# Attention of four batches and scores of the next four in one block on TensorE

## The chip, the cores and the metric

The kernel runs on one core of a Trainium2 chip. The metric is the device time of one execution in microseconds. It is the median of several runs. One further execution was taken by the hardware profiler, and the views quoted below are of that one. Engines are named as in the profile: PE is TensorE (PEld its weight loads), DVE is VectorE, ACT is ScalarE, POOL is GpSimd, SP is the engine whose queue issues nearly all DMAs.

## What is computed

Two layers over 128 batches of a 128 x 512 matrix, all in fp32. The first takes a maximum over the features of adj x; the second is attention with 8 heads of 64 features, masked by the adjacency, with a projection and a layer norm.

```python
# layer 0: A = C - b = adj @ x, so out = max(0, max(A, axis=-1) + b); one value a row
x = layernorm(x + layer0(x))
# layer 1
q, k, v = split(x @ w_qkv)                    # 8 heads of 64
attn = softmax(where(adj == 0, -inf, q @ k.T * 64 ** -0.5))
o = (attn @ v) @ w_proj + b_proj
x = layernorm(x + o + layernorm(o) * ln_gamma + ln_beta)
```

(In the reference layer 0 adds A at one feature to C - A at another; C - A is the bias b, since A and C use the same adjacency.)

## The kernel before

**Tiling.** Four batches are a group (G = 4, 32 groups). A batch is 128 rows, so one batch's matrix fills the 128 partitions. The projections q and k together, v, and the output projection o of a group are done as "units": a unit is a matrix product of 512 tokens by 512 columns in seven products of half size (Strassen's scheme in Winograd's form) instead of eight. `product(i)` (L171) is eight matmuls of 128 x 128 weights by 256 columns. Products 1, 6 and 7 go into PSUM bank b1, one added on top of the other, 2 into b2, 5 and 3 into b3, 4 into b4. `snap(k)` (L184) is a copy of b1 by ScalarE after product 1, 6 or 7; `result(half, col)` (L202) is an addition by VectorE of a bank and a snap, into SBUF: (0, 0) reads b2, (0, 1) b3, (1, 0) b4, and (1, 1) b3, before product 3 is added to it. The sums that the scheme needs of the operands are made by GpSimd (`x_sums`, `o_sums`, `weight_sums`), in the beginning also by VectorE.

**Attention of a batch.** `scores(b)` (L396) is 16 matmuls with 64 rows of the array, in pairs, even heads into one bank and odd heads into another; `softmax_max` (L407) scales and masks the two banks into an SBUF tile s and takes the maximum of each head; `softmax_exp` (L425) is eight exponentials on ScalarE; `softmax_div` (L439) divides; `prob_transpose` and `prob_write` (L447, L457) transpose in blocks of 32 and write to DRAM, and `prob_read` (L466) reads back into a tile pT with the transposition finished. `attend(b)` (L482) is 16 matmuls with 64 columns of the array, in pairs, into one bank; `attend_copy` (L496) copies that bank out by ScalarE.

**The main loop** (L806) has 60 steps; step p does two batches, a = 2p and b = 2p + 1. Each step begins on TensorE with a block, `attend(a - 2)`, `attend(b - 2)`, `scores(a)`, `scores(b)`. After that come the seven products of `first` (a half of the q and k columns of the next group), two layer-0 products `l0_mm` and the seven products of `second`. In even steps (ph = 0) `second` is the output projection of the group before; in odd steps it is v of the next group. Product 3 of a unit is issued in the course of the next unit (`before.product(3)`). All 8 PSUM banks are in use: b1 to b4 by the units, pss0 and pss1 by scores and later in the step by `l0_mm`, po and pa by attention and by the second batch's scores.

**The order.** It is written out by hand: every instruction is pinned to the program's order on its engine, so each engine runs its instructions in exactly the order of the source. A tile with a tag has that tag's slots; an instruction that first writes a new tile in a slot waits until the last reader of the old one is done. After the loop the last eight batches are written out one by one; the beginning, before the loop, does layer 0 of the first groups.

## Time and profile before

| what | us |
|---|---|
| median of three runs | 1952.45 |
| lowest and highest | 1952.12, 1953.76 |
| the profiled execution, its own time | 1953.87 |
| span of its profile | 1951.6 |
| mean granted clock of TensorE | 0.998 |

In a view of the timeline a line has the start, the time to the last end, engine, line of the kernel, operation, what it writes and reads, shapes, how many in a row, and in brackets how long the engine was idle before, and what ended this. Ends of matmuls are modelled, as these are pipelined: what one costs is seen from one start to the next. The lines named L77 and L74 are those of helpers, so groups are told apart by their tiles: b_qk, b_v and b_o are the banks of the three kinds of unit, po an attention, pss scores, pa a layer-0 product, pt a transpose on TensorE.

| group | number | mean ns |
|---|---|---|
| masking of scores, a bank (L411) | 256 | 682 |
| division of a softmax (L77) | 128 | 1978 |
| copy of an attention bank (L501), median | 128 | 586 |
| snap of q and k (L186) | 192 | 586 |
| result of q and k (L77) | 256 | 675 |

### The profile page before, as it was taken

Reading aid. Unit: us, or ns where it says so; the run is one execution under the profiler, and the core shown is the slowest. Engines: PE = TensorE matmul, PEld = TensorE weight load, DVE = VectorE, ACT = ScalarE, POOL = GpSimd, SP = SyncE. Lnnn points to the kernel's source line nnn. Section 1 sums busy time; section 2 is a strip of 40 time slices with the busy share of each in tenths; the row PEclk is TensorE's granted clock in tenths of the full one; section 3 lists DMA queues with packets and bytes.
Section 4 is the critical chain, followed back from the end, with each engine's and each line's share of the span. In section 5 each row is a group of like instructions: output and inputs, shape, how many; then the busy total and the mean of one; then the engine's idle time right before and its main releaser. Section 6 shows DMA issues by size and latency. Waiting matters only on the chain.

```text
span 1951.6 us, 33053 instructions
## 1 busy us (share of the span) xinstructions
PE 1937.1 (99%) x11541; PEld 1638.4 (84%) x11541; DVE 1560.6 (80%) x2514; ACT 1065.2 (55%) x3095; POOL 1293.7 (66%) x823
## 2 busy tenths in 40 slices
PE   9999999999999999999999999999999999999998
PEld 6888888888888888888888888888888888888885
DVE  6767878778788787787887877877878778778787
ACT  3544655545546555555465555554655555546566
POOL 6336666767667676676776676766767666767648
PEclk9999999999999999999999999999999999999999
DMA  7647566575665665756756657657667576675574
GB/s 221 167 127 182 146 190 169 166 206 151 174 193 157 190 170 165 206 151 174 198 156 187 175 161 205 161 166 193 159 186 179 167 195 162 166 204 154 157 227 141
DMA packets 444934, 341.74 MB, mean 175 GB/s; under 512 B 276832, under 2 KB 378336, under 8 KB 444768
## 3 DMA queue, kind: packets, MB, share of 16 engines
q1 hardware_dynamic: 444336, 338.85, 63.6%
q8 instruction: 91, 1.49, 0.3%
q10 hardware_dynamic: 432, 0.79, 0.2%
q14 instruction: 75, 0.61, 0.1%
HBM read 172.82 MB, written 166.72 MB: 174 GB/s over the span
## 4 chain that ended last, share of the span: by engine, by line
PE 95%; DVE 2%; POOL 1%; ACT 1%; DMA 0%; issue 0%; SPq 0%; POOLq 0%; ACTq 0%; DVEq 0%
PE b_qk L74 40%; PE b_v L74 19%; PE b_o L74 18%; PE pss L74 6%; PE po L74 6%; PE pa L74 5%; DVE st_mv_last L261 0%; POOL zl L77 0%; DMA x<-in_x_dram 0%; ACT s L430 0%; POOL s_o L77 0%; DVE amax L297 0%; DVE mv_last L262 0%; DVE o L77 0%; DVE pu L451 0%
## 5 line engine op out<-in xcount | busy, mean ns | idle before, releaser
L74 PE MATMUL b_qk<-s_x,wqk 128*128 128x256 f32 x2048 | 473.6, 379 | 1.0 <-DVE qk L77 0.8
L74 PEld LDWEIGHTS b_qk<-s_x,wqk 128*128 128x128 f32 x2048 | 388.8, 190 | 55.4 <-DVE qk L77 1.5
L430 ACT ACTIVATE s<-s,nmax 128x128 f32<-128x128 f32 x1024 | 396.2, 391 | 5.3 <-DVE nmax L423 5.3
L74 PE MATMUL b_qk<-x1T,wqk 128*128 128x256 f32 x1536 | 360.2, 384 | 0.1
L74 PEld LDWEIGHTS b_qk<-x1T,wqk 128*128 128x128 f32 x1536 | 287.9, 191 | 45.5 <-issue 1.0
L77 POOL TENSOR_TENSOR z<-z,ga_bc 128x1024 f32<-128x1024 f32 x58 | 164.6, 2837 | 167.0 <-ACT z L284 167.0
L275 POOL TENSOR_SCALAR rs_mv<-mv 128x6 f32<-128x6 f32 (+2 forms) x61 | 14.8, 242 | 385.8 <-DVE mv L262 385.8
L77 DVE TENSOR_TENSOR s<-s,rec 128x1024 f32<-128x1024 f32 x128 | 253.2, 1978 | 4.4
L186 ACT COPY u_qk<-b_qk 128x512 f32<-128x512 f32 x192 | 112.5, 586 | 243.3 <-PE b_qk L74 242.4
L74 PE MATMUL b_v<-wv,s_x 128*128 128x256 f32 x1024 | 237.0, 379 | 0.0
L74 PE MATMUL b_o<-wp,s_o 128*128 128x256 f32 x992 | 229.6, 379 | 0.2 <-ACT u_o L186 0.2
L74 PEld LDWEIGHTS b_v<-wv,s_x 128*128 128x128 f32 x1024 | 194.4, 190 | 26.9 <-ACT u_v L186 0.4
L411 DVE SCALAR_TENSOR_TENSOR s<-pss,mask 128x512 f32<-128x512 f32 x256 | 164.1, 682 | 61.4 <-PE pss L74 61.2
L74 PEld LDWEIGHTS b_o<-wp,s_o 128*128 128x128 f32 x992 | 188.2, 190 | 26.4 <-issue 0.8
L77 DVE TENSOR_TENSOR qk<-b_qk,u_qk 128x512 f32<-128x512 f32 x256 | 167.9, 675 | 48.5 <-PE b_qk L74 44.5
L77 POOL TENSOR_TENSOR x<-x,be_bc 128x1024 f32<-128x1024 f32 x64 | 181.3, 2835 | 33.1 <-DVE rec L441 27.4
L430 ACT ACTIVATION_READ_ACCUMULATOR s<-s,nmax 128x1 f32 x1024 | 194.6, 190 | 0.0
L77 DVE TENSOR_TENSOR v<-b_v,u_v 128x512 f32<-128x512 f32 x127 | 86.1, 679 | 133.8 <-PE po L74 128.9
L186 ACT COPY u_o<-b_o 128x512 f32<-128x512 f32 x91 | 53.3, 586 | 238.7 <-PE b_o L74 238.7
L186 ACT COPY u_v<-b_v 128x512 f32<-128x512 f32 x95 | 55.7, 586 | 233.1 <-PE b_v L74 233.1
L74 PE MATMUL b_v<-wv,x1T 128*128 128x256 f32 x768 | 176.5, 379 | 0.0
L74 PEld LDWEIGHTS b_v<-wv,x1T 128*128 128x128 f32 x768 | 145.8, 190 | 32.3 <-issue 13.9
(129 smaller groups left out, 3399.6 us busy)
## 6 DMA issues: line engine op xcount, KB each, us to landing
hop<-pu SPq DMA_DIRECT2D x128, 512.0 KB, 3.6
pT<-hop SPq DMA_DIRECT2D x512, 128.0 KB, 3.7
spill<-x SPq DMA_DIRECT2D x64, 512.0 KB, 4.8
x<-in_x_dram SPq DMA_DIRECT2D x62, 512.0 KB, 4.4
xhop<-xt SPq DMA_DIRECT2D x248, 128.0 KB, 2.3
x1T<-xhop SPq DMA_DIRECT2D x248, 128.0 KB, 3.9
xr<-spill SPq DMA_DIRECT2D x59, 512.0 KB, 3.6
out_dram<-xr SPq DMA_DIRECT2D x58, 512.0 KB, 4.1
```

The costliest lines, as they stand in the source:

```text
L74: pin(nc.tensor.matmul(*args, **kwargs))
L77: pin(eng.tensor_tensor(dst, a, b, op))
L186: pin(nc.scalar.copy(t, self.banks[1]))
L275: pin(nc.gpsimd.tensor_scalar(rs[:, :n], mv[:, :n, 1], EPS, None, ALU.add))
L411: nc.vector.scalar_tensor_tensor(s[:, par], pss[b][par], SCALE, mask.unsqueeze(1).to_broadcast([P, NP, P]), ALU.mult, ALU.add,)
L430: nc.scalar.activation(prob[b][:, i], prob[b][:, i], AF.Exp, bias=nmax[b][:, i : i + 1], accum_out=psums[b][:, i : i + 1],)
```

## The change

In steps with p > 1 the block comes in even steps only. `group_block` issues the attention of the four batches of the group before, each into the next of the banks po, pa, pss0, pss1, and then the scores of all four batches of the new group, into b2 and b1, b4 and the first free bank, two free banks, and the last free bank and b2 again. `group_mask` masks all four on VectorE, with the maximum of the first batch between. Odd steps take the maxima of the last two batches, from the s tiles that were masked before. The step p = 2 attends two batches only, since p = 1 keeps its own block. After the loop, the last even step has the same block, and the scores of L - 5 and L - 4 in the middle of it are gone.

In an even step `first.product(2)` comes after `before.product(3)`, the two results there change places, the exponentials of b come after `first.snap(2)`, and `first.result(1, 1)` and `(1, 0)` come before `softmax_div(b)`.

Tiles: v has 4 slots (2 groups) instead of 2; s and pT share 4 slots (they had 2 each); the second half of q and k has 2 slots instead of 3; the transposed x (xt) has one instead of two. The last two s tiles lie in the place of the q and k weights.

In the beginning the sums of the weights are issued in another order (two of them ahead of a statistic), batch 2 is normalised by VectorE instead of ScalarE, product 2 comes before the transposes of batches 2 and 3, the results of the first unit come before a group of statistics, and products 4 and 5 of the next unit change places.

```diff
-    def softmax_max(b):
-        s = sb.tile([P, 2, NP, P], F32, tag="s", name=f"s_{b}", bufs=2)
-        for par in range(2):
+    def softmax_mask(b, order=(0, 1), place=None):
+        s = place or sb.tile([P, 2, NP, P], F32, tag="s", name=f"s_{b}", bufs=4)
+        for par in order:
...
+    def softmax_max(b):
+        if b in pss:
+            softmax_mask(b)
         nmax[b] = small.tile([P, H], F32, tag="nmax", name=f"nmax_{b}")
...
+    weight_sums(wqk, 0, HE, 2)
+    mv = stats("first_2", ("y", 2), ("y", 3), fused=1)
+    rs, _ = stat_of.pop(("y", 2))
+    pin(nc.vector.tensor_scalar(xs[2], xs[2], mv[:, 0, 0:1], rs, ALU.subtract, ALU.mult))
+    l0_norm(3)
...
     cur.product(1)
     cur.snap(1)
+    cur.product(2)
     for f in range(2, G):
         l0_transpose_pe(f)
-    cur.product(2)
...
+    before.snap(3)
+    l0_add(2 * G - 1)
+    before.result(1, 1)
+    before.result(1, 0)
     stats("second", *(("y", f) for f in range(G, 2 * G)))
     weight_sums(wv, 0, HE)
-    before.snap(3)
-    before.result(1, 1)
-    before.result(1, 0)
...
+    def group_block(old):
+        a = old[-1] + 1
+        free = ["po", "pa", "pss0", "pss1"]
+        for t in old:
+            attend(t, free[0])
+            attend_copy(t)
+            free.append(free.pop(0))
+        banks = ("b2", "b1"), ("b4", free[0]), (free[1], free[2]), (free[3], "b2")
+        for k in range(G):
+            scores(a + k, banks[k])
+
+    def group_mask(a):
+        softmax_mask(a)
+        softmax_mask(a + 1)
+        softmax_max(a)
+        softmax_mask(a + 2)
+        softmax_mask(a + 3, (1, 0))
...
-        if p > 0:
-            attend(a - 2)
-            before.snap(3)
-            attend_copy(a - 2)
-            attend(b - 2, "pa")
-            attend_copy(b - 2)
+        before.snap(3)
+        if p == 1:
+            for t, tag in ((0, "po"), (1, "pa")):
+                attend(t, tag)
+                attend_copy(t)
             scores(a)
             scores(b, ("po", "pa"))
-        else:
-            before.snap(3)
+        if p > 1 and ph == 0:
+            group_block(range(2 if p == 2 else a - G, a))
         before.result(1, 1)
...
         if p > 0:
             softmax_max(b)
             first.product(1)
             first.snap(1)
-            first.product(2)
+            if p == 1 or ph:
+                first.product(2)
             softmax_exp(a)
...
+        if p > 1 and ph == 0:
+            before.product(3)
+            first.product(2)
+            before.result(0, 1)
+            first.result(0, 0)
+        else:
+            first.result(0, 0)
+            before.product(3)
+            before.result(0, 1)
...
         if p > 0:
             first.snap(3)
-        else:
+        if p == 0 or ph == 0:
             first.result(1, 1)
             first.result(1, 0)
         softmax_div(b)
```

## The prediction

> **What bounds the kernel now.** I read the page first (sections 1 and 4), then the timeline of TensorE over one step of the main loop, then the other engines at the same place, then the waits of TensorE.

> ```profile
> PE 1937.1 (99%) x11541; PEld 1638.4 (84%) x11541; DVE 1560.6 (80%) x2514; ACT 1065.2 (55%) x3095; POOL 1293.7 (66%) x823
> PE 95%; DVE 2%; POOL 1%; ACT 1%; DMA 0%; issue 0%; SPq 0%; POOLq 0%; ACTq 0%; DVEq 0%
> ```

> TensorE is busy 1937.1 of 1951.6 us, and 95% of the chain that ended last is its own. Of its waits the longest is one of 1.7 us at the beginning; in the loop there are none. So only two things count: TensorE time that goes away, and waits that the new order gives to TensorE. The first is found in an even step (p even, its block at 645.44):

> ```profile
> 643.62 1.89 PE L74 MATMUL b_v<-wv,s_x 128*128 128x256 f32 x8
> 645.44 1.97 PE L74 MATMUL po<-pT,v 128*64 128x128 f32 x32
> 647.34 2.06 PE L74 MATMUL pss<-qk 64*128 64x128 f32 x32
> 649.32 3.72 PE L74 MATMUL b_qk<-x1T,wqk 128*128 128x256 f32 x16
> 652.88 1.89 PE L74 MATMUL b_v<-wv,s_x 128*128 128x256 f32 x8
> ```

> Eight projection matmuls take 1.726 us from start to start (649.32 to 652.88 is one switch and 16 of them; 16 without a switch take 3.45). From 643.62 + 1.726 = 645.35 to 652.88 - 3.45 = 649.43 the two attentions and two scores take 4.08 us. Inside, they run in pairs, 0.110 and 0.112 us apart (22 and 24 records in two short windows: (1.37 - 0.27)/10 and (1.51 - 0.28)/11):

> ```profile
> 615.74 1.37 PE L74 MATMUL po<-pT,v 128*64 128x128 f32 x22
> ...
> 617.69 1.51 PE L74 MATMUL pss<-qk 64*128 64x128 f32 x24
> ```

> 16 x 0.1093 + 16 x 0.1117 = 3.54 us (the means to one more digit). The other 0.55 us are the three changes of tile shape: 128x128 to 128x64, to 64x128, and back.

> [...] The trace agrees: 0.14, 0.20 and 0.20 us. [...] the division of a softmax (two SBUF inputs) takes 1.23 us alone, and 1.88 beside GpSimd, where it ends 1.08 us after GpSimd's instruction does; GpSimd's product then takes 3.34 instead of 2.37:

> ```profile
> 656.36 1.27 POOL L77 TENSOR_TENSOR s_o<-oT,s_o 128x512 f32<-128x512 f32 x1
> 657.59 3.34 POOL L77 TENSOR_TENSOR z<-z,ga_bc 128x1024 f32<-128x1024 f32 x1
> 661.00 3.23 POOL L77 TENSOR_TENSOR z<-z,o 128x1024 f32<-128x1024 f32 x1
> 664.31 2.35 POOL L77 TENSOR_TENSOR xr<-xr,z 128x1024 f32<-128x1024 f32 x1
> 666.62 2.35 POOL L77 TENSOR_TENSOR x<-x,be_bc 128x1024 f32<-128x1024 f32 x1
> ```

> ```profile
> 61.29 1.23 DVE L77 TENSOR_TENSOR s<-s,rec 128x1024 f32<-128x1024 f32 x1
> ...
> 656.83 1.88 DVE L77 TENSOR_TENSOR s<-s,rec 128x1024 f32<-128x1024 f32 x1
> ```

> **Part 1, fewer blocks.** Before, p = 2 to 59 have 58 blocks; after, the even ones alone, 29. Each block removed saves 0.55: -15.9 us. The scores that stood alone in the end (1853.51) join a block too: in and out of that shape, about -0.4. All other matmuls stay.

> **Part 2, the odd step loses its cover.** Products 1, 6 and 7 of a unit share bank b1. The last thing that an even step gives TensorE is second.product(7); the first in an odd step from p = 3 on is now first.product(1), into the same bank, which ScalarE must first copy out (before.snap(3)). Until now the block lay between the two. Elsewhere the two products with the adjacency (l0_mm) or, without these, the order (2, 1) separate them.

> ```profile
> 645.60 0.59 ACT L186 COPY u_v<-b_v 128x512 f32<-128x512 f32 x1 [4.60 <-PE b_v L74]
> ```

> Product 7 starts its last matmul at 645.13, which ends at 645.51; the copy runs 645.60 to 646.19. TensorE could start at 645.35, and starts about 0.1 after the copy: 0.94 us of wait. After a wait the first matmul is slower, too. Both can be seen in the two waits of this kind in the trace: it goes on 0.05 us after VectorE's 70.29 and 0.14 after ScalarE's 1917.20, and its eight matmuls take 0.10 and 0.08 more:

> ```profile
> 70.35 1.99 PE L74 MATMUL b_qk<-s_x,wqk 128*128 128x256 f32 x8 [0.23 <-DVE v L77]
> ...
> 1917.34 1.97 PE L74 MATMUL b_o<-wp,s_o 128*128 128x256 f32 x8 [0.24 <-ACT u_o L186]
> ```

> 1.03 us (0.97 to 1.09; a wait can't gain) x 29 odd steps = +29.9 us. Queued behind it is the whole TensorE stream; nothing else hides it.

> **Part 3, the even step.** The new block takes 4 x (0.875 + 0.893) + 0.55 = 7.6 us, so first.product(1) starts at 652.87 instead of 649.43. Do its banks come free? snap(3) ends 646.19, result(1,1) and (1,0) at 647.5 (V is held for two groups, so they no longer wait for the attention); b4 is wanted at 650.1. The four attention copies end by 649.9; their banks are wanted from 650.1 on. The first mask starts 650.25 and frees b2 at 650.9; the fourth score wants it at 651.9. VectorE then does eight masks (0.605 apart) and the first maximum (1.14): the last but one mask frees b2 at 655.7, and first.product(2), moved behind before.product(3) (652.87 + 1.83 + 1.73), wants it at 656.4. It fits by 0.7 us; if VectorE were later, each us beyond costs 29 us.

> Then TensorE runs products 2, 6, 5, 4, 7; the last matmul of 7 starts at 664.84, snap(3) ends at 665.9. Here is the second new wait. first.result(1,1) and (1,0) are moved ahead of softmax_div(b), so VectorE, done with the first batch (about 664.9), waits for snap(3), and all the following comes after: two results 1.17, reciprocal 0.20, division 1.26, transpose 1.17, two statistics of o 1.61, two l0_max 1.66, first.result(0,1) 0.68. From 665.94 that is 673.69, and second.product(5), into the bank b3 that this result reads, is wanted at 664.84 + 8.84 = 673.68 (the same distance as 661.30 to 670.14 now). So it just fits if the division is undisturbed. It is disturbed: GpSimd's chain keeps its times up to 657.59; there z x gamma, no longer beside a division, ends at 659.95, z + o at 662.4 (it holds the first division, ready at 660.4, back to 663.5), the sum into xr starts then and ends 665.9, and l0_beta runs 665.95 to 668.3. The second division, due at 667.3, ends at 668.3 + 1.08 instead of 668.55: 0.8 to 0.9 late; 1.4 if the first division comes before z + o (they are 0.35 apart). With 0.16 for restarting and slower first matmul: 1.0 or 1.5, taken 1.1, bounds 0 and 1.6. The order before had results behind both transposes, with VectorE at work from 654 to 667.7 and 0.87 spare. For p = 4 to 58 (p = 2 has no o statistics): 28 x 1.1 = +30.8 us (0 to 45).

> In the odd step VectorE has four masks less, and by the same sum no later bank is late.

> **Part 4, the beginning.** Now the transposes of batches 2 and 3 wait 1.71 us for their normalisation, and in the clock window after that gap TensorE is granted half speed: 16 matmuls from 18.68 take 4.91 instead of 3.45.

> ```profile
> 17.25 1.63 PE L327 MATMUL pt<-ident,x 128*128 128x128 f32 x8 [1.71 <-ACT x L284]
> 18.68 5.07 PE L74 MATMUL b_qk<-x1T,wqk 128*128 128x256 f32 x16
> ```

> ```profile
> 14.79:18.20 3.41, 1.65 (x10) 0.98 (x9) 0.60 (x3) 1.82 (x3) 2.99 (x5) 1.00 1.06 377
> 18.20:21.62 3.42, 3.42 (x11) 2.84 (x10) 3.06 (x4) 0.17 (x1) 3.34 (x3) 0.50 0.74 237
> 1939.90:1943.32 3.42, 2.47 (x7) 0.92 (x6) 3.32 (x8) 2.52 (x4) 2.99 (x7) 1.00 0.35 129
> ```

> (Columns: length, busy time of TensorE, weight loads, VectorE, ScalarE, GpSimd, then clock.) Product 2, which needs neither, now fills the gap; product 4 starts when the transposes are copied, near 19.45 instead of 21.86: -2.4. Statistics moved behind result(1,1) take away the 0.79 wait at 36.6 and its slow first matmul, -0.9. I take -3.0 (-1 to -4). GpSimd's sums are the same eight.

> **At nothing:** the mask and copy counts are unchanged; SP issues the same DMAs in the same queue order, and an even step's probabilities now have a step more to land. One xt buffer is refilled a step later, 30 us against 2.3 to landing. The s and pT tiles share four buffers: each pT follows its own s. The end I take as moved as a whole, 0 (+-1).

> **Sum** against the profiled execution's own 1953.87 (span 1951.6): -15.9 - 0.4 + 29.9 + 30.8 - 3.0 = +41.4, so 1995.3. It lies 1.4 above the median of the runs, 1952.45; for that the forecast is **1994**.

> **Rivals.**
> - Only the wait for b1: GpSimd is over a us later or earlier than I place it, or VectorE has slack. For it: 0.87 spare now. Against: l0_beta covers the due time by 1.3 us before and 1.0 after. -19.3 + 29.9: **1963**.
> - Faster: the odd step's start costs nothing, because something that I overlook keeps b1 free, and the b3 wait stays under 0.1. Place: second.product(7) to first.product(1); it decides where that wait is below 0.55 us. Against: a copy of 0.59 us after the last matmul's end is needed in any case. -19.3: **1933**.
> - The clock: [...] 1.65 us busy in such a window cost half the clock of the next, 2.47 did not; a wait of 1.1 leaves 2.3, which no run shows. If it trips in every second step: 29 x 1.7 more, **2043**.
> - The b3 wait without that for b1: 1964.

> **Chances.** Both waits 0.52 (own range 1984 to 2008), b1 alone 0.26, clock 0.09, faster 0.08, b3 alone 0.03, about even 0.02. Faster or slower is told from 0.2% (3.9 us) on: faster 0.08, within 0.02, slower 0.90. The range 1958 to 2010 takes in the first two and the last but one; the clock and the faster case are left out.

> **What would show it.** Right: in the waits of TensorE, b_qk behind ACT u_o 29 times, about 0.9 each, and b_o behind DVE qk 28 times, about 1; 31 blocks of po; first.product(2) behind no DVE s. Wrong: no wait where an odd step begins, or a b2 wait in the new block, or clock windows of 0.5 in the loop.

## The result and the profile after

The changed kernel takes 2061.28 us (four runs, 2057.43 to 2061.96) where the kernel before takes 1952.73 beside it: 1.0552 times as long, with a 95% interval from 1.0539 to 1.0565. It was forecast slower, at 1994 with 2010 as the upper end; the loss of 108.6 us is 2.6 times the 41.4 us that the sum had. The first two lines are from the page of the profiled execution after (2061.92 us, span 2060.1); the next two are from its list of TensorE's waits (total us, number, longest).

```profile
PE 1968.9 (96%) x11541; PEld 1661.0 (81%) x11541; DVE 1564.4 (76%) x2515; ACT 1056.5 (51%) x3094; POOL 1262.0 (61%) x823
...
PE 78%; DVE 17%; ACT 2%; POOL 1%; issue 1%; DMA 0%; ACTq 0%; POOLq 0%; SPq 0%; DVEq 0%
```

```profile
PE b_o L75 <- DVE qk L78: 55.2, 28, 2.0
PE b_qk L75 <- ACT u_o L187: 21.7, 29, 1.0
```

Both forecast waits are there, in the forecast places and numbers: 29 at the beginning of the odd steps, behind ScalarE's copy, and 28 in the even steps, behind the result that frees b3. VectorE now holds 17% of the chain, which was 2%. But TensorE is also busy 32 us longer than before, with the same 11541 matmuls and less switching. The timeline of TensorE from the end of an even step to the beginning of an odd one shows all three:

```profile
700.78 1.89 PE L75 MATMUL b_o<-wp,s_o 128*128 128x256 f32 x8
704.63 2.67 PE L75 MATMUL b_o<-wp,s_o 128*128 128x256 f32 x8 [1.96 <-DVE qk L78]
707.09 2.94 PE L75 MATMUL b_o<-wp,oT 128*128 128x256 f32 x8
709.87 1.89 PE L75 MATMUL b_o<-wp,s_o 128*128 128x256 f32 x8
712.49 3.72 PE L75 MATMUL b_qk<-x1T,wqk 128*128 128x256 f32 x16 [0.73 <-ACT u_o L187]
```

Product 6 begins at 700.78, so product 5 could follow 1.73 later, at 702.50; it starts at 704.63. That is a wait of 2.13 us, not 1.0 to 1.5 (the bracket says 1.96 because a matmul's end is modelled later than the next could start; read starts against starts). Products 5 and 4, 2.67 and 2.94 long instead of 1.89, run partly at half clock. Then product 7 starts at 709.87, product 1 of the odd step could start at 711.60, and starts at 712.49: 0.89 us.

The half clock is in the table of stretches (length, busy time of TensorE, weight loads, VectorE, ScalarE, GpSimd, granted clock, DMA share, GB/s). The stretches are windows of 3.41 us on the grid on which the clock's records of this profile change:

```profile
702.39:705.80 3.41, 1.45 (x7) 1.06 (x6) 3.30 (x8) 1.98 (x3) 0.00 (x0) 1.00 0.97 254
705.80:709.21 3.41, 3.41 (x9) 2.66 (x8) 2.63 (x8) 0.00 (x0) 0.67 (x2) 0.50 1.09 291
1149.53:1152.94 3.41, 1.49 (x7) 1.34 (x8) 3.27 (x10) 1.98 (x3) 0.00 (x0) 1.00 0.95 235
1152.94:1156.36 3.42, 3.42 (x18) 3.02 (x17) 2.35 (x7) 0.00 (x0) 1.00 (x2) 1.00 1.08 311
```

The first window holds the whole wait, and the next one runs at half clock; the third holds 1.92 us of a wait as long, cut by the window's edge, and the clock stays. Twenty of the 28 waits are followed by a window at half clock. Such a fall of the clock after a wait is called a trip below. From one block of attentions to the next, a pair of steps takes 64.32 us with a trip and 62.63 us without, so a trip costs 1.69 us.

Why is the wait twice what was forecast? VectorE's timeline before the result, and GpSimd's beside it:

```profile
694.75 1.29 DVE L78 TENSOR_TENSOR qk<-b_qk,u_qk 128x512 f32<-128x512 f32 x2 [2.08 <-ACT u_qk L187]
695.96 0.19 DVE L448 RECIPROCAL rec<-sums 128x8 f32<-128x8 f32 x1
696.19 3.25 DVE L78 TENSOR_TENSOR s<-s,rec 128x1024 f32<-128x1024 f32 x1
699.47 1.25 DVE L458 STREAM_TRANSPOSE pu<-s 128x1024 f32<-128x1024 f32 x1
```

```profile
685.49 1.27 POOL L78 TENSOR_TENSOR s_x<-x1T,s_x 128x512 f32<-128x512 f32 x1 [1.52 <-PE b_v L75]
...
693.69 2.36 POOL L78 TENSOR_TENSOR xr<-xr,z 128x1024 f32<-128x1024 f32 x1
696.01 2.35 POOL L78 TENSOR_TENSOR x<-x,be_bc 128x1024 f32<-128x1024 f32 x1
```

VectorE is idle for 2.08 us, waiting for snap(3); the wait was forecast, at about 1.0. The division then takes 3.25 us: GpSimd began its addition of ln_beta 0.18 us before it, and the division ends 1.08 us after that addition (699.44 and 698.36). With the addition left out, in a run below, it takes 1.23. In the forecast that addition lay 1.2 us earlier against the block. What delayed GpSimd stands in the bracket: its last x sum waits 1.52 us for TensorE. The sum overwrites an operand of before.product(3). That product now starts 9.25 us after the block's start (683.52 less 674.27) instead of 7.44 (652.88 less 645.44 in the kernel before): the block is 3.5 us longer, and first.product(2), 1.73 us, no longer stands ahead of it.

### The profile page after: what moved, and what is told of

It reads as the page before. It is cut to its first block, busy times and chain, and to the rows that moved or that the text cites. A ratio compares the mean times of both kernels' runs of the same rounds, so it can differ in the third digit from the quotient of the medians.

```text
span 2060.1 us, 33371 instructions
## 1 busy us (share of the span) xinstructions
PE 1968.9 (96%) x11541; PEld 1661.0 (81%) x11541; DVE 1564.4 (76%) x2515; ACT 1056.5 (51%) x3094; POOL 1262.0 (61%) x823
## 4 chain that ended last, share of the span: by engine, by line
PE 78%; DVE 17%; ACT 2%; POOL 1%; issue 1%; DMA 0%; ACTq 0%; POOLq 0%; SPq 0%; DVEq 0%
PE b_qk L75 34%; PE b_v L75 18%; PE b_o L75 12%; PE pss L75 6%; PE po L75 5%; DVE s L78 5%; DVE qk L78 3%; PE pa L75 3%; DVE pu L458 2%; DVE amax L298 2%; DVE st_mv L262 2%; ACT u_o L187 1%; ACT u_qk L187 1%; DVE r L300 1%; DVE mv L263 1%
## 5 line engine op out<-in xcount | busy, mean ns | idle before, releaser
L437 ACT ACTIVATE s<-s,nmax 128x128 f32<-128x128 f32 x1008 | 390.2, 393 | 3.4 <-DVE nmax L430 3.4
L75 PE MATMUL b_o<-wp,s_o 128*128 128x256 f32 x992 | 257.5, 407 | 55.6 <-DVE qk L78 55.2
L75 PEld LDWEIGHTS b_o<-wp,s_o 128*128 128x128 f32 x992 | 196.8, 201 | 94.7 <-DVE qk L78 66.4
L78 DVE TENSOR_TENSOR s<-s,rec 128x1024 f32<-128x1024 f32 x126 | 259.1, 2057 | 4.3
L414 DVE SCALAR_TENSOR_TENSOR s<-pss,mask 128x512 f32<-128x512 f32 x252 | 156.5, 683 | 84.3 <-PE pss L75 84.3
L78 POOL TENSOR_TENSOR z<-z,ga_bc 128x1024 f32<-128x1024 f32 x58 | 136.9, 2361 | 129.7 <-ACT z L285 129.7
L75 PEld LDWEIGHTS b_o<-wp,oT 128*128 128x128 f32 x744 | 154.7, 208 | 38.4 <-issue 13.8
L75 PE MATMUL b_o<-wp,oT 128*128 128x256 f32 x744 | 185.3, 402 | 0.3 <-ACT b_o L552 0.3
L303 ACT ACTIVATE x<-x,r 128x512 f32<-128x512 f32 x128 | 92.0, 721 | 175.6 <-DVE r L300 166.8
L78 DVE TENSOR_TENSOR o<-b_o,u_o 128x512 f32<-128x512 f32 (+1 forms) x123 | 80.5, 676 | 133.0 <-ACT u_o L187 105.0
```

The source lines that it names most:

```text
L75: pin(nc.tensor.matmul(*args, **kwargs))
L78: pin(eng.tensor_tensor(dst, a, b, op))
L303: pin(nc.scalar.activation(xs[f], xs[f], AF.Identity, bias=rr.pop(f)))
L414: nc.vector.scalar_tensor_tensor(s[:, par], pss[b][par], SCALE, mask.unsqueeze(1).to_broadcast([P, NP, P]), ALU.mult, ALU.add,)
L437: nc.scalar.activation(prob[b][:, i], prob[b][:, i], AF.Exp, bias=nmax[b][:, i : i + 1], accum_out=psums[b][:, i : i + 1],)
```

## The experiments

The theory after the result: the two waits come from two places in the order (product 1 first in odd steps; the results ahead of the second division in even ones), the length of the second from GpSimd, and the half clock from that length. The rivals: VectorE is overloaded by eight masks in even steps, whatever the order; and the clock falls for another reason than the gap. All edits are made to the changed kernel unless it says otherwise.

### The two orders, one at a time and together

```diff
+            if p > 1 and ph:
+                first.product(2)
             first.product(1)
             first.snap(1)
-            if p == 1 or ph:
+            if p == 1:
                 first.product(2)
```

> The changed kernel with one edit: odd steps from p = 3 on begin with product 2 (bank b2) and then product 1 (bank b1), as elsewhere in the kernel. Theory: the 29 waits for b1 (0.89 us and 0.10 for the slower first matmul each) go, about 29 us, so 2032 us; the 28 waits for b3 stay at about 2.1 us each and the clock still falls in some 20 windows. Rival (ScalarE's copy is late for product 6 as well, so the wait only moves by a product): 2055 to 2061.

Measured: 2004.67 us, ratio 1.0263 (1.0248 to 1.0278). The 29 waits are gone, so they don't move to another product. But the kernel is 57 us faster, and both expectations had missed: the waits for b3 are unchanged,

```profile
PE b_o L75 <- DVE qk L78: 55.1, 28, 2.0
```

while the windows of half clock in the loop fall from 20 to 3. The granted clock of that profile is 0.996 after 0.982. The reason is arithmetic with the lengths of these two profiles. Without the first wait a pair of steps takes 61.63 us, which is 18.06 windows of 3.413. So the wait for b3 moves by only 0.06 of a window from pair to pair, and, by an estimate from these lengths, the edge of a window cuts it in the 25 of the 28 waits that trip nothing. It trips at 315.5 (the clock granted from 314.20 to 317.60 is 0.69), 871.9 and 1428.3, every nine pairs (9 x 61.63 + 1.69 = 556.4); each trip puts the waits off by half a window (1.69 of 3.413). With both waits a pair takes 62.63 or 64.32 us, 18.35 or 18.84 windows, and 20 of the 28 waits had 2.01 us or more in one window. Some 28 us of the gain are the waits, some 29 the 17 trips fewer.

```diff
-        if p == 0 or ph == 0:
+        if p == 0:
             first.result(1, 1)
             first.result(1, 0)
         softmax_div(b)
...
-        if ph == 1:
+        if p > 0:
             first.result(1, 1)
             first.result(1, 0)
```

> The changed kernel with one edit: in even steps first.result(1, 1) and (1, 0) come after softmax_div(b) and prob_transpose(b) again. Theory: the b3 wait comes from that order, so all 28 waits of second.product(5) go (2.13 us and 0.10 each, 62 us), and with them the 20 windows of half clock (1.7 us each, 34 us): 1964 us. Rival (VectorE is simply overloaded in even steps by the eight masks, whatever the order): a wait of over 1 us stays at the same place, 2010 or more. A second rival for the clock (it falls because the matmuls are denser, not because of the gap): waits go, windows of half clock stay, 1998.

Measured: 1964.48 us, ratio 1.0061 (1.0046 to 1.0076), the expected number. No wait for b3 is left, and no window of half clock in the loop (granted clock 0.999 after 0.982); the wait for b1 stays as it was:

```profile
PE b_qk L75 <- ACT u_o L187: 21.7, 29, 1.0
```

VectorE has the same masks to do in this kernel, so the rival of the overloaded VectorE falls; and TensorE now runs its matmuls with fewer gaps and at that higher clock, so the rival that denser matmuls lower the clock falls too.

Then with both edits, the two diffs above:

> Both edits at once, the order of products in odd steps and the place of the results in even steps. Theory: nothing is left of the two waits and of the half clock; what stays is the saving on changes of tile shape (16.3 us) and that of the beginning (2 us): 1935 us. Rival (the saving on the changes of shape is taken back elsewhere, for instance at bank b2 in the new block): 1945 to 1953.

Measured: 1936.51 us, ratio 0.9915 (0.9899 to 0.9932): faster than the kernel before by 16.0 us. In its page and in the timeline at an odd step TensorE goes from product 7 (669.35) to products 2 and 1 (16 matmuls at 671.08) without a gap:

```profile
PE 1920.1 (99%) x11541; PEld 1638.0 (85%) x11541; DVE 1550.9 (80%) x2515; ACT 1060.3 (55%) x3094; POOL 1285.4 (66%) x823
```

```profile
669.35 1.89 PE L75 MATMUL b_o<-wp,s_o 128*128 128x256 f32 x8
671.08 3.62 PE L75 MATMUL b_qk<-x1T,wqk 128*128 128x256 f32 x16
```

This is the best version of the study. The block of four and four is worth having once it no longer uncovers the two waits.

### The clock alone

```diff
         second.snap(2)
+        if ph == 0 and p > 3:
+            fill = psum.tile([P, 2 * P], F32, tag="po", name=f"fill_{p}")
+            for _ in range(8):
+                pe(fill, lhsT=zeros[:, :P], rhs=zeros, start=True, stop=True)
         second.product(5)
```

> The changed kernel, with eight matmuls of zeros into the free bank po ahead of second.product(5) in even steps from p = 4 on: 1.73 us of work whose result nobody reads, put into the wait for b3. Theory: the wait for the bank keeps its length, but TensorE is busy in it, so no window of half clock comes in the loop: 34 us less, 2027 us, granted clock 0.998. Rival (the clock doesn't depend on the gap): the same 2061 us or some us more, and 20 windows of half clock stay.

Measured: 2061.55 us with a granted clock of 0.999 and no window of half clock in the loop. By the time alone the rival had won; by the clock it had lost. The timeline shows the mistake: the eight calls are sixteen matmuls in the trace, 3.45 us, and longer than the wait they were to fill.

```profile
700.15 1.89 PE L75 MATMUL b_o<-wp,s_o 128*128 128x256 f32 x8
701.88 3.62 PE L75 MATMUL fill<-zeros 128*128 128x256 f32 x16
705.33 1.89 PE L75 MATMUL b_o<-wp,s_o 128*128 128x256 f32 x8
```

The same with half of it:

```diff
-            for _ in range(8):
+            for _ in range(4):
```

> As the kernel with the filled wait, with half of the filling: four calls of matmul are eight matmuls of 0.216 us, 1.73 us in a wait of 2.13. In the kernel before this they were sixteen, 3.45 us, longer than the wait by 1.3 us (28 x 1.3 = 36 us more), with no window of half clock (34 us less), which together gave the same time. Theory: now the clock's part alone goes, 34 us: 2027 us. Rival (what the filling took from the clock it didn't give to the time): 2055 or more.

Measured: 2028.30 us, ratio 1.0387 (1.0373 to 1.0401). The wait is still there, filled up to its last 0.3 us (6.9 us in 28 waits), the granted clock is 0.998, and the time is 33.0 us shorter. So the clock's part is 33 us, near 20 x 1.69, and the gap is its cause: product 5 still starts 3.85 us after product 6 (704.63 less 700.78 there, 694.51 less 690.66 here), and nearly every pair of steps takes the 62.63 us of a pair without a trip.

```profile
PE b_o L75 <- DVE qk L78: 6.9, 28, 0.3
```

### What makes the second wait long

```diff
             l0_write(n)
-            l0_beta(n)
+            if ph == 1 or p < 4:
+                l0_beta(n)
```

> The changed kernel without l0_beta (GpSimd's addition of ln_beta to a pair of batches) in even steps from p = 4 on; that part of the computation is left out. Theory: VectorE's second division waits there for GpSimd's l0_beta, 3.25 us in place of 1.26; without it the result that frees b3 comes 2.0 us earlier and the wait of second.product(5) shrinks from 2.13 to about 0.15 us. 28 x 2.0 = 56 us and the 20 windows of half clock, 34 us: 1971 us. Rival (VectorE is late by its own queue, and GpSimd is beside the point): the division is shorter by less than 0.5 us, 2045 or more.

Measured: 1971.21 us, ratio 1.0095 (1.0080 to 1.0111), as expected. This kernel leaves ln_beta out in even steps. The second division takes 1.23 us, and no wait for b3 is left in the list:

```profile
669.23 1.23 DVE L78 TENSOR_TENSOR s<-s,rec 128x1024 f32<-128x1024 f32 x1
```

But the kernel is still 6.7 us above the one with the results back (1964.48). A wait too short for the list is left: products 6 and 5, 16 matmuls, take 3.66 us here (673.82 to 677.48) and 3.45 there (671.46 to 674.91). The first two lines are of the kernel without the addition, the last two of the one with the results back:

```profile
673.82 3.82 PE L75 MATMUL b_o<-wp,s_o 128*128 128x256 f32 x16
677.48 1.89 PE L75 MATMUL b_o<-wp,oT 128*128 128x256 f32 x8
```

```profile
671.46 3.62 PE L75 MATMUL b_o<-wp,s_o 128*128 128x256 f32 x16
674.91 1.89 PE L75 MATMUL b_o<-wp,oT 128*128 128x256 f32 x8
```

So the new order by itself costs 0.2 us a step: VectorE's queue all but fits, as the sum in the prediction had it. The other 2.0 us of the wait are the difference between the division beside GpSimd's addition, 3.25 us, and without it, 1.23.

```diff
+            if p > 1 and ph == 0:
+                before.product(3)
             first.product(1)
             first.snap(1)
...
         if p > 1 and ph == 0:
-            before.product(3)
             first.product(2)
```

> The changed kernel with before.product(3) as the first product after the block in even steps, ahead of first.product(1). Theory: GpSimd's last x sum no longer waits 1.52 us for that product, so l0_beta comes some 1.3 us earlier and releases the second division that much earlier: the wait for b3 is about 0.9 us (the prediction's case), no window of half clock. 28 x 1.3 = 36 us and 34 us: 1990 us. Rival (GpSimd's delay has another cause, its additions being slower beside VectorE): the wait stays at 2.1 us, 2055 to 2065.

Measured: 1984.70 us, ratio 1.0163 (1.0149 to 1.0176). With before.product(3) one product earlier GpSimd's waits for it go from 33 to 5. These are the lines of the lists of GpSimd's waits, first of the changed kernel, then of this one:

```profile
POOL s_x L78 <- PE b_v L75: 54.5, 33, 5.2
```

```profile
POOL s_x L78 <- PE b_v L75: 10.5, 5, 5.2
```

The division then takes 1.74 us instead of 3.25, and TensorE's wait is 0.61 us from start to start (677.89 + 1.73 to 680.23), 0.45 in the bracket:

```profile
673.30 1.74 DVE L78 TENSOR_TENSOR s<-s,rec 128x1024 f32<-128x1024 f32 x1
```

```profile
680.23 1.99 PE L75 MATMUL b_o<-wp,s_o 128*128 128x256 f32 x8 [0.45 <-DVE qk L78]
```

No window of half clock is left in the loop (granted clock 0.999). But for the place of before.product(3), this is the kernel that the prediction's sum described, with both waits and GpSimd on time: it was put at 1994, and takes 1985.

### The beginning alone

The kernel before with the beginning of the changed one: the hunks ahead of the loop, and the place of l0_norm in step 0. Its core, against the kernel before:

```diff
+    weight_sums(wqk, 0, HE, 2)
+    mv = stats("first_2", ("y", 2), ("y", 3), fused=1)
...
+    cur.product(2)
     for f in range(2, G):
         l0_transpose_pe(f)
-    cur.product(2)
...
+    before.snap(3)
+    l0_add(2 * G - 1)
+    before.result(1, 1)
+    before.result(1, 0)
     stats("second", *(("y", f) for f in range(G, 2 * G)))
```

> The kernel before with the new beginning alone (order of the weight sums, batch 2 normalised by VectorE, product 2 ahead of the transposes, results ahead of the second statistics, products 4 and 5 exchanged). By the first attention in the two profiles (75.73 and 73.71 us) it saves 2.0 us: 1950.5 us. The prediction's sum had 3.0: 1949.5 us. Rival (the loop takes it back, as its first transfers set the start): 1952.5 us.

Measured: 1951.57 us, ratio 0.9992 (0.9984 to 1.0000), about 1 us less, at the edge of what can be told: the interval reaches from -3.1 to 0 us. The profiles show no later loss. From the first attention to the end the one of this kernel takes 1875.8 us (72.87 to 1948.7) and the one of the kernel before 1875.9 (75.73 to 1951.6). What differs is the start itself, by 2.9 us here and by 2.0 between the kernels before and after. Each of these is one execution, and that of the kernel before was 1.4 us above its median, so the medians are the better measure.

## Why the prediction was wrong

| term | forecast | measured | from |
|---|---|---|---|
| fewer changes of tile shape | -16.3 | -15.1 | both orders mended, against the beginning alone |
| beginning | -3.0 | -1.1 | the beginning alone, against before |
| wait for b1, 29 | +29.9 | +28.0 | results back, against both orders mended |
| wait for b3, 28 | +30.8 | +63.1 | odd order, against both mended, less 3 windows of half clock |
| half clock, 20 windows | 0 | +33.0 | the filled wait, against the changed kernel |
| sum | +41.4 | +107.9 | (changed less before: 108.6) |

**Right:** the direction and the mechanism of both waits, with their places and numbers. The cost of the tile shapes, 0.55 us a block, holds within 1.2 us over the kernel: a pair of steps takes 59.94 us before and 59.39 with both orders mended. The wait for b1 has 0.89 us and about 0.1 for the slower first matmul; 1.03 was forecast and 0.97 came. In the new block the banks came free as placed: from the first attention to product 1 it is 7.42 us (674.27 to 681.69; forecast 7.43), and no wait for b2 appears. The division was due 21.92 us after the block's start (21.87 forecast).

**Wrong, the step that failed:** "GpSimd's chain keeps its times up to 657.59", in part 3. The chain was followed through VectorE's reads and ScalarE's copies, but not through TensorE: before.product(3) was moved, and the write that waits for its reads, run_sums(xsums[3:]), was not asked for. It waits 1.52 us, and GpSimd's product z x gamma starts 13.68 us after the block's start instead of 12.15. The addition of ln_beta then starts 0.18 us before the second division instead of 1.36 before it, and the division takes 2.0 us longer than without that addition (3.25 against 1.23). The term was 1.1 us a step and is 2.25; the bounds given, up to 1.6, didn't hold it either. The first division did come before z + o (689.27 and 690.39), which the prediction had as its dearer case, 1.4; they fell short all the same, because they came from the order of GpSimd's instructions and not from their waits. With the wait taken away the term is 0.6 to 0.7, so the taken 1.1 had also been somewhat too high.

**Wrong, the second term:** the clock, a rival with a chance of 0.09 and 49 us, is 33 us. It is not independent of the first mistake. In the loop of the changed kernel the clock fell after no window with less than 2.01 us of gap; a wait of 1.1 us stays well below that, and the waits of 2.13 tripped it 20 times in 28. Windows of half clock in the loop were among the prediction's own signs of being wrong. The two errors are one error and its consequence, and the chances treated them as separate.

**Perhaps off in size:** the beginning, -3.0 against -1.1; with an interval from -3.1 to 0 the forecast isn't excluded. The forecast counted what TensorE no longer waits before its first attention. The profile of the changed kernel has a new wait of 0.74 us there, at 48.4; that of the beginning alone has not, so how much it takes back stays open.

## What to carry to other kernels

When a block of work is moved off a place, list what stood on both sides of it: here two products of one bank became neighbours, and the copy between them, 0.6 us that nothing had shown, was on the path 29 times. Follow a moved matmul not only to who reads its result but to who wants to overwrite its operands. And price a wait in two parts: its own length, and the slower matmuls that can come after it; here 20 waits of 2.13 us were each followed by a window at half clock, at 1.69 us apiece. Where a long wait can't be removed, a matmul of zeros in it can save the second part: 33 us here.

## What the runs showed of the hardware

A division of a softmax took 1.23 us with no addition of GpSimd beside it. Beside one of 2.35 us that began 0.18 us before it in the changed kernel it took 3.25, and beside one of 2.36 that began 1.70 before it, with before.product(3) first, 1.74. Both times the division ended 1.08 us after the addition.
